# A fifth batch's keys and values computed early, at the border between two decoder layers

## The chip, the cores and the metric

The kernel runs on one core of one Trainium2 chip. A core has a matrix engine (TensorE, called PE in the profile; its weight loads are PEld), a vector engine (VectorE, DVE), an activation engine (ScalarE, ACT), a general engine (GpSimd, POOL) and a sync engine (SyncE, SP) that mostly issues transfers. Each engine works through its own queue in order, and semaphores tie the queues together. Sixteen DMA engines move data between the device memory (HBM) and the on-chip memories: SBUF with 128 partitions, and PSUM, in eight banks, into which PE writes. The metric is the device time of one execution, in microseconds; less is better.

## The reference

A decoder of two layers in single precision, on 16 batches of 112 tokens with 256 features; a context of 375 rows per batch feeds the cross-attentions. Cut to what matters here:

```python
x = x + attn0(ln(x))                      # layer 0: linear attention
x = x + xattn0(ln(x), ctx)                # layer 0: cross-attention
x = x + moe0(ln(x))                       # layer 0: top-2 of 16 experts, and a shared one
x = x + attn1(ln(x), W_qkv, W_out)        # layer 1: softmax self-attention, 16 heads of 64
x = x + xattn1(ln(x), ctx)                # layer 1: cross-attention, 8 heads of 64
x = x + moe1(ln(x))                       # layer 1: top-2 of 8 experts, with a capacity

def xattn1(x, context):
    xn = layer_norm(x, g1, b1); cn = layer_norm(context, g2, b2)
    q = xn @ Wq
    k, v = split(cn @ Wkv, 2)             # Wkv: 256 x 1024
    return softmax(q k^T / 8) v @ Wout + bout
```

The keys and values of xattn1 depend on the context and on weights alone, not on x. They can be computed at any time before the second cross-attention reads them.

## The kernel before

The whole decoder is one program in stages. Activations `x` stay in SBUF (112 tokens on the partitions, 16 batches); `xnT` holds the normalised, transposed input of the running stage, 128 x 2 x 1792. `w_all` is one large SBUF region, cut into weights by hand; its third part, from 2*WR, holds in turn the weights of layer 0's attentions, the key and value weights `Wkv` of xattn1, and the q, k and v weights of attn1.

**Batches computed ahead.** Four batches, `AHEAD` (line 359), have their keys and values for xattn1 computed during layer 0. The pieces are `c_ahead` (three PE transposes of the context for one half of its features, and an ACT evacuation with scale and bias), `k_ahead` (one of four key pieces: two matmuls of 375 columns, an ACT copy) and `v_ahead` (one of three value pieces: two matmuls of 512 columns, an ACT copy). After the last piece ACT's queue writes the result to device memory (`kd`, `vd`). `norm_ahead` normalises the context on DVE. A list `ahead` holds these pieces, and `take` puts some of them between the routing steps and the shared expert of layer 0, where PE would wait.

**The expert blocks.** Layer 0's expert rows are sorted into blocks of 128 rows. `blocks` (line 1143) runs 36 of them as a pipeline: `fetch` loads rows five blocks ahead, `turn` transposes, `up` multiplies, `turn_act` transposes the activation, `down` multiplies and scatters the rows back to device memory (`yo`) with an indirect transfer from POOL. `fetch` also starts the three weight loads of attn1, behind the rows of blocks 12, 17 and 22.

**The join.** Behind the 36 blocks every engine loads the number of blocks that the routing needs and branches (lines 1161 and 1162): only if there are more than 36, the conditional block runs the rest. Behind it, the first instructions of each engine wait for what went before, the scattered rows among it.

**Layer 1.** `combine` (line 1528) loads a batch's two expert rows per token, DVE adds them to `x`, `norm_one` normalises (DVE, POOL) and transposes (PE) them into `xnT`. After the first two batches come nine pieces of q, k and v projections, and then 32 units of self-attention. While they run, contexts and pieces for the first batch that is not in `AHEAD` are made ready.

**The second cross-attention.** `units` is a list of 32 half batches (four heads each). In each turn PE transposes the weights of the current half (`turned`), computes the scores of the next (`scores`: DVE takes the maxima, ACT the exponentials, DVE the reciprocals, POOL the division, line 1484), and multiplies by the values. Between these it makes what the next batch needs: if that is not in `AHEAD`, two `c_piece`, four `k_piece` and three `v_piece` (the same work as the pieces ahead, line 1421 on); if it is, two loads from `kd` and `vd` through SP (`k_load`, `v_load`).

**What sets the order.** Within a block `manual_schedule` the named engines run in the order of the code: PE and DVE in layer 0's routing and blocks, PE alone in layer 1. The other engines' queues, SP's transfers among them, are ordered by a planner at build time, from estimated durations and dependencies. `issue_after` keeps a transfer behind another one on the same queue.

## Time and profile before

| | us |
|---|---|
| median of 3 runs | 1604.29 |
| lowest and highest run | 1603.69, 1607.48 |
| the profiled execution's own time | 1611.35 |
| its span, first to last instruction | 1609.6 |

The mean granted clock of PE in the profiled execution is 0.973 of full speed. By the trace, the expert blocks run from 546.8 to 608.4 us, the self-attention from about 640 to 948, the second cross-attention from there to about 1314.

In the lines of the profile, PE's busy time comes with the number of its instructions; a single-precision matmul of the program shows as two. `L120` is the helper `mm_sum`, so matmuls are told apart by their tiles. A row of stretches gives for each stretch its length, the busy time of PE, PEld, DVE, ACT and POOL, the granted share of PE's clock, the mean busy share of the DMA engines, and GB/s. A row of the timeline gives start, duration, engine, line, operation, tiles, the number of instructions merged, and in brackets the idle time before and what ended it.

### The profile page before, as it was taken

The page shows a single profiled execution, that of the slowest core. Times are in us where ns is not written, and L with a number is a line of the kernel's source. Part 1 is how long each engine was busy: PE and PEld are TensorE (multiplying, and loading weights), DVE is VectorE, ACT ScalarE, POOL GpSimd, SP SyncE. Part 2 cuts the span into 40 slices and gives each one's busy share as a digit, 9 for nine tenths or more (in the row PEclk, how much of TensorE's full clock was granted, in tenths as well). Part 3 has the DMA queues.
Part 4 walks back from the last instruction along what each step waited for, and adds up shares of the span by engine and source line. Part 5 has one row for each costly group of instructions (what it writes and reads, how often), then busy time and mean ns, then how long its engine had stood idle before and what let it go on. Part 6 is the DMA issues. An engine that isn't in the chain of part 4 may idle for free.

```text
span 1609.6 us, 30346 instructions
## 1 busy us (share of the span) xinstructions
PE 1501.8 (93%) x11438; PEld 1127.5 (70%) x11438; DVE 964.1 (60%) x2649; ACT 577.9 (36%) x1437; POOL 483.1 (30%) x647
## 2 busy tenths in 40 slices
PE   7898999999988896899999989999999978999998
PEld 5776777777754585778888756666666657788786
DVE  6986777777762353976677655566575566342124
ACT  3441444444442252223333233343434323333332
POOL 5642122222115352323333344544445420000000
PEclk9999999999999897999999999999999988999999
DMA  6500322222224476200000010101010012344421
GB/s 170 143 10 21 94 67 65 67 65 65 64 76 158 130 231 214 54 24 1 1 1 2 20 56 10 49 20 48 19 30 30 1 53 79 137 178 157 147 89 48
DMA packets 84929, 116.52 MB, mean 72 GB/s; under 512 B 13433, under 2 KB 70946, under 8 KB 84778
## 3 DMA queue, kind: packets, MB, share of 16 engines
q1 hardware_dynamic: 78690, 98.25, 20.1%
q0 software_dynamic: 3312, 8.54, 1.6%
q10 hardware_dynamic: 2776, 7.72, 1.4%
q8 instruction: 95, 1.56, 0.4%
q14 instruction: 56, 0.46, 0.1%
HBM read 84.41 MB, written 22.08 MB: 66 GB/s over the span
## 4 chain that ended last, share of the span: by engine, by line
PE 76%; DVE 13%; POOL 4%; DMA 3%; issue 2%; another core or an unknown queue 1%; ACT 1%; SPq 0%; POOLq 0%; DVEq 0%; ACTq 0%
PE pT L120 49%; PE pT L785 3%; PE pT L1461 3%; PE pT L1493 2%; POOL pr L1484 2%; DVE mx L769 2%; PE pT L1509 2%; PE pT L803 2%; PE pT L767 2%; PE pT L1358 2%; PE pT L1393 2%; PE pT L1379 2%; PE pT L620 1%; DVE st L234 1%
## 5 line engine op out<-in xcount | busy, mean ns | idle before, releaser
L1484 POOL TENSOR_SCALAR pr<-pr,den 112x375 f32<-112x375 f32 x128 | 157.0, 1244 | 176.9 <-DVE den L1482 157.7
L120 PE MATMUL pT<-xnT,w_all 128*128 128x224 f32 (+2 forms) x800 | 165.3, 358 | 0.6 <-DVE xnT L269 0.5
L120 PEld LDWEIGHTS pT<-xnT,w_all 128*128 128x128 f32 x800 | 145.9, 197 | 10.2 <-issue 5.7
L794 ACT ACTIVATE pr<-pT 125x336 f32<-125x336 f32 x256 | 94.6, 456 | 126.3 <-PE pT L785 126.3
L769 DVE TENSOR_REDUCE mx<-pT 112x1 f32<-112x375 f32 x256 | 122.2, 539 | 11.3 <-PE pT L767 9.9
L1371 POOL TENSOR_TENSOR pr<-pr,den 112x448 f32<-112x448 f32 x64 | 59.9, 956 | 198.8 <-DVE den L1369 147.9
L120 PE MATMUL pT<-w_all 128*128 (+3 forms) x376 | 113.1, 453 | 1.7 <-ACT w_all L392 0.8
L120 PE MATMUL pT<-w_all,cT 128*125 128x256 f32 (+1 forms) x336 | 111.4, 475 | 0.0
L120 PE MATMUL pT<-cT,w_all 128*128 128x375 f32 x320 | 110.2, 486 | 0.0
L120 PE MATMUL pT<-w_all,xnT 128*112 128x256 f32 (+1 forms) x320 | 105.7, 477 | 1.9 <-ACT xnT L566 0.9
L120 PE MATMUL pT<-w_all,oT 128*112 128x256 f32 x448 | 106.4, 383 | 0.6 <-DVE oT L1400 0.6
L242 POOL TENSOR_SCALAR nr<-nmv 112x1 f32<-112x1 f32 x96 | 22.3, 232 | 273.7 <-DVE nmv L235 273.1
L1308 ACT COPY pT<-pT 112x448 f32<-112x448 f32 (+1 forms) x64 | 34.0, 532 | 170.9 <-PE pT L1493 88.3
L120 PEld LDWEIGHTS pT<-w_all 128*128 128x128 f32 (+2 forms) x376 | 70.2, 190 | 33.8 <-issue 4.6
L1473 ACT ACTIVATE pr<-pT,top 112x375 f32<-112x375 f32 x128 | 72.4, 572 | 56.8 <-DVE top L1472 54.4
L120 PEld LDWEIGHTS pT<-cT,w_all 128*128 128x128 f32 x320 | 59.3, 190 | 41.1 <-issue 5.8
L120 PEld LDWEIGHTS pT<-w_all,oT 128*112 128x112 f32 x448 | 75.7, 177 | 16.3 <-DVE oT L1400 1.0
L120 PE MATMUL pT<-first_in,w_all 128*128 128x192 f32 x512 | 86.6, 329 | 0.0
L120 PEld LDWEIGHTS pT<-first_in,w_all 128*128 128x128 f32 x512 | 84.4, 192 | 1.5 <-issue 0.3
L120 PEld LDWEIGHTS pT<-w_all,cT 128*125 128x125 f32 x336 | 61.1, 187 | 33.3 <-issue 22.7
L120 PEld LDWEIGHTS pT<-w_all,xnT 128*112 128x112 f32 x320 | 57.1, 183 | 35.8 <-issue 22.4
L1767 DVE SCALAR_TENSOR_TENSOR hT<-pT,vT,gt 128x192 f32<-128x192 f32 x64 | 26.7, 417 | 90.5 <-ACT gt L1766 90.4
(306 smaller groups left out, 3019.2 us busy)
## 6 DMA issues: line engine op xcount, KB each, us to landing
w_all<-in_L_ffn_w_c_fc_dram SPq DMA_DIRECT2D x12, 1024.0 KB
w_all<-in_L_ffn_w_gate_dram SPq DMA_DIRECT2D x12, 1024.0 KB
w_all<-in_L_ffn_w_c_proj_dram SPq DMA_DIRECT2D x12, 1024.0 KB
cx<-in_ctx_dram SPq DMA_DIRECT2D x32, 375.0 KB
kz<-kn SPq DMA_DIRECT2D x128, 46.9 KB
xg<-w_all SPq DMA_DIRECT2D x1, 5547.0 KB
xb<-xg SPq DMA_DIRECT2D x36, 129.0 KB
yb<-yo SPq DMA_DIRECT2D x16, 224.0 KB
```

Source lines behind the costliest of these rows:

```text
L120: mm(o, l, r, start=(i == 0), stop=(i == len(terms) - 1))
L767: mm(ps[i][:L, :S], qz[b % 2][r, g, :], kz[b % 2][r, g, :], start=True, stop=True)
L769: nc.vector.tensor_reduce(mx[b % 2][:, g, i, 16:17], ps[i][:L, :S], AX.X, ALU.max, negate=True)
L785: mm(pw[i][:KC, j * L : (j + 1) * L], kz[b % 2][r, g, j * KC : (j + 1) * KC], qm[r, :], start=True, stop=True,)
L794: nc.scalar.activation(pr[:, i, :], pw[i][:KC, : NKC * L], AF.Exp)
L803: mm(po[32 * i : 32 * i + 32, :L], va[b % 2][:, j, 4 * g + i, :], pr[:, i, j * L : (j + 1) * L], start=(j == 0), stop=(j == NKC - 1),)
L1308: nc.scalar.copy(dst, src)
L1358: mm(ps[k][:L, s * L : (s + 1) * L], q, kk, start=True, stop=True)
L1371: nc.gpsimd.tensor_tensor(pr[:, k], pr[:, k], bcast(den[:, k, :], L), ALU.mult)
L1461: mm(ps[2 * s + k][:L, :S], qTs[b // 2][rows(k), m, (b % 2) * L : (b % 2 + 1) * L], kTs[b][rows(k), m, :], start=True, stop=True,)
L1473: nc.scalar.activation(pr[:, i, :], ps[i][:L, :S], AF.Exp, bias=top[:, i : i + 1], scale=1.0, accum_out=den[:, i : i + 1],)
L1484: nc.gpsimd.tensor_scalar(pr[:, n, :], pr[:, n, :], den[:, n : n + 1], None, ALU.mult)
```

## The change

Batch 2 becomes the fifth batch computed ahead. It is not worked into the list `ahead`; its pieces are placed by hand.

- Its context is loaded by `ctx_ahead`, which already runs for the index 4 after the transposes of the third batch. It is normalised on DVE in turn 30 of the block pipeline, and transposed in turns 36 and 37, where no new block begins.
- The key and value weights are needed once more, and attn1's weights have replaced them in `w_all`. They are loaded a second time (1 MB), behind block 24's rows, into the last 1024 columns of each half of `xnT`, which nobody needs until layer 1 reaches those batches.
- Two key pieces stand behind the 36 blocks, ahead of the branch; two key pieces and the three value pieces stand behind the conditional block, in a region in which PE's order is the code's, ahead of layer 1. ACT's queue writes keys and values out, as for the other four.
- In the second cross-attention batch 2 is no longer projected but loaded, during batch 1, and the contexts that are fetched there are those of the other eleven batches.

```diff
-    AHEAD = (0, 4, 8, 12)
+    AHEAD = (0, 4, 8, 12, 2)
...
                 kap[0].tile([128, 2, S], F32, tag="acT", name="acT", bufs=1)
-                if i % 2
+                if i % 2 or i == 4
...
-        mm_sum(pk[:, :S], [(wkv_a[0][:, c, m * 128 : (m + 1) * 128], acTs[i][:, c, :]) for c in range(2)])
+        mm_sum(pk[:, :S], [(wkv_a[i // 4][:, c, m * 128 : (m + 1) * 128], acTs[i][:, c, :]) for c in range(2)])
...
-        mm_sum(pv[:KC, :], [(acTs[i][:, c, j * KC : (j + 1) * KC], wkv_a[0][:, c, 512:]) for c in range(2)])
+        mm_sum(pv[:KC, :], [(acTs[i][:, c, j * KC : (j + 1) * KC], wkv_a[i // 4][:, c, 512:]) for c in range(2)])
...
-        for i in range(len(AHEAD))
+        for i in range(4)
...
-            + [lambda i=i, c=c: c_ahead(i + 1, c) for c in range(2)] * (i + 1 < len(AHEAD))
+            + [lambda i=i, c=c: c_ahead(i + 1, c) for c in range(2)] * (i < 3)
...
+                    if j == 24:
+
+                        wkv_a.append(xnT[:, :, NT - 1024 :])
+                        with tc.issue_after(got.ins):
+                            nc.sync.dma_start(wkv_a[1], rows_of(t["L1_xattn_Wkv"]))
...
+                    if begin == 0 and n == stop - 6:
+                        norm_ahead(4)
+                    if begin == 0 and n in (stop, stop + 1):
+                        c_ahead(4, n - stop)
...
             blocks(0)
+            for m in range(2):
+                k_ahead(4, m)
         n_used = nc.values_load(used[0:1, 0:1], min_val=0, max_val=NB0)
         with tc.If(n_used > NB_MEAN):
...
+        with tc.manual_schedule(engines={mybir.EngineType.PE}):
+            for m in range(2, 4):
+                k_ahead(4, m)
+            for j in range(NKC):
+                v_ahead(4, j)
```

## The prediction

> **What bounds the kernel now.** I read the page first. TensorE (PE) is busy 93% of the span and carries 76% of the chain that ended last, so work taken off PE counts where PE sets the pace, and work put on it is free only where it stands idle.

> ```profile
> span 1609.6 us, 30346 instructions
> PE 1501.8 (93%) x11438; PEld 1127.5 (70%) x11438; DVE 964.1 (60%) x2649; ACT 577.9 (36%) x1437; POOL 483.1 (30%) x647
> ...
> PE 76%; DVE 13%; POOL 4%; DMA 3%; issue 2%; another core or an unknown queue 1%; ACT 1%; SPq 0%; POOLq 0%; DVEq 0%; ACTq 0%
> ```

> Then the stretches of the layers' border. PE works 1.24 us of the 14.9 us after the last expert block, and at half the clock for most of it; the next stretch starts at half clock too, with the DMA engines full.

> ```profile
> 608.40:623.30 14.90, 1.24 (x4) 0.58 (x4) 4.26 (x14) 0.47 (x1) 4.56 (x8) 0.59 0.43 135
> 623.30:640.00 16.70, 16.66 (x66) 14.16 (x67) 4.57 (x12) 2.80 (x5) 1.58 (x4) 0.85 1.03 369
> ```

> The timeline of PE and POOL says what the gap is, and the waits (us, times, longest) who holds it.

> ```profile
> 606.93 0.33 PE L1126 MATMUL pT<-call,sg 128*128 128x128 f32 x1
> 607.10 1.27 PE L1133 MATMUL pT<-w_all,aT 128*128 x4
> 620.98 0.61 PE L267 MATMUL pT<-call,xn 112*128 112x112 f32 x2 [12.61 <-DVE nmv L235]
> 622.22 0.63 PE L267 MATMUL pT<-call,xn 112*128 112x112 f32 x2 [0.64 <-DVE xn L238]
> 623.34 8.70 PE L120 MATMUL pT<-xnT,w_all 128*128 128x224 f32 x32 [0.48 <-DVE xnT L269]
> ```

> ```profile
> 610.40 0.96 POOL L1063 DMA_INDIRECT yo<-os,to  x1 [0.30 <-issue]
> ```

> ```profile
> SPq L1530 <- DMA yo<-os,to: 13.6, 1, 13.6
> ```

> The last scatter of expert rows lands at 613.16; every engine's first instruction behind the conditional block is released within 0.02 us of that. This is the join: nothing behind it starts earlier, whatever it depends on. Then come the gather (landed 616.66), adds, norm, and the first projections at 623.34.

> Last, the second cross-attention, cut from one batch's scores to those of two batches later. Odd lines end up with a batch whose successor is projected in place, even lines with one whose successor's keys and values are loaded (4, 8, 12).

> ```profile
> 980.20:1027.00 46.80, 46.80 (x285) 30.64 (x284) 24.62 (x59) 18.75 (x53) 21.03 (x20) 1.00 0.12 35
> 1027.00:1068.75 41.75, 38.77 (x256) 26.27 (x255) 21.51 (x54) 15.98 (x47) 21.00 (x20) 0.96 0.08 28
> 1068.75:1117.70 48.95, 48.95 (x299) 32.95 (x298) 34.69 (x115) 19.84 (x58) 21.54 (x20) 1.00 0.12 33
> 1117.70:1160.20 42.50, 40.62 (x263) 27.73 (x262) 23.05 (x59) 16.95 (x51) 21.00 (x20) 0.96 0.07 27
> 1160.20:1209.10 48.90, 48.90 (x299) 32.63 (x298) 33.75 (x112) 19.56 (x56) 21.48 (x20) 1.00 0.12 33
> 1209.10:1250.70 41.60, 39.65 (x266) 27.18 (x264) 23.46 (x62) 17.48 (x53) 21.22 (x20) 1.00 0.07 27
> ```

> PE is never idle where the successor is projected, and idle 2 to 3 us where it is loaded. The pieces that move are these (start, us):

> ```profile
> 981.65 0.86 PE L1430 MATMUL pT<-call,cx 125*128 125x125 f32 x6
> ...
> 985.59 2.69 PE L120 MATMUL pT<-cT,w_all 128*128 128x375 f32 x8
> 988.12 1.88 PE L120 MATMUL pT<-w_all,cT 128*125 128x512 f32 x4
> ...
> 1044.73 0.97 PE L1493 MATMUL pT<-call,pr 112*125 112x112 f32 x3 [0.63 <-POOL pr L1484]
> 1045.63 2.69 PE L1461 MATMUL pT<-kt,qt 64*112 64x375 f32 x8
> ```

> From start to start, six context transposes take 0.70 us, two key pieces 2.53, one value piece 1.75 (1.81 alone, 3.43 for two). One batch is 0.70 + 5.06 + 5.24 = 11.0 us of PE.

> **The change part by part.**

> 1. *Extra transfers among the expert blocks.* One more 1024 KB load of the key/value weights, issued by SP behind block 24's rows, and batch 2's context earlier. The three weight loads already there stand at 560.37, 568.51 and 576.64; around the last, two up-projections of a block take 1.11 and 0.96 us instead of 0.87, 0.33 together, and nothing else moves, since rows are fetched five blocks (8.1 us) ahead. I take 0.1; from 0 to 2.7 us (1 MB at the 380 GB/s of the border burst, were none of it covered).

> 2. *Normalising batch 2's context on DVE at block 30.* Three operations of 0.32 us. DVE idles 0.75 us in each 1.63 us block and each block's pieces are spread over four turns: 0, covered by that idle time; without it 0.96.

> 3. *Context transposes in the last two turns.* 0.70 us of PE and two ScalarE (ACT) evacuations of some 0.5 us (the neighbouring 128x375 copies take 0.47), between the last gated outputs. What they may delay is the last output on ACT (608.41 to 608.88), which POOL takes only at 610.40, as its scatters follow each other every 1.26 us. POOL is elsewhere 0.59 us behind ACT, so 0.93 us is cover. I take 0.1, up to 0.7.

> 4. *Two key pieces ahead of the join.* 2.53 us of PE from about 609.0 to 611.6, the copy by 612.1, then ACT's own load of the block count (0.47) and branch: about 1 us of cover before 613.16, since SP's first gather also waits for ACT to have passed. 0; if the order on ACT eats the cover, the join is up to 0.7 late.

> 5. *Two key and three value pieces behind the join.* PE passes a row of semaphore waits from 613.19 to about 614.3, then has 2.53 + 5.24 = 7.77 us of work ahead of the first transposes, which would be ready at 620.98 and 622.22. So this part is not fully hidden. PE's clock: after an idle stretch from 611.6 to 614.3 I count one granted-clock window at half, 3.41 us (the trace's half-clock stretches are multiples of it), that is 1.7 us lost. PE is through at 614.3 + 7.77 + 1.7 = 623.8, the four transposes and their copies take it to 624.8, 1.5 later than 623.34. But the projections now run at full clock: in the profile 623.34 to 628.19 was at half, 4.85 us, worth 2.4. Border: 1.5 - 2.4 = -0.9. Ends: clock never falls, -2.6; half clock through the whole stack (15.5 us instead of 9.5), +5.1.
> [...]

> 6. *Writing the keys and values out.* Two transfers of 750 KB from ACT's queue at about 619 and 624, into the burst (share 1.03) that loads the next weights. 1.5 MB at 380 GB/s ends it 3.9 us later, near 644; the first thing behind it on SP, batch 4's gathered rows, is used at 648.4. 0; from there on up to 3.9 if it isn't covered. ACT has nothing else between 609 and 626.8.

> 7. *Second cross-attention: batch 2 is loaded, not projected.* 11.0 us of PE go, but not as time. With little PE work a half batch waits for the scores' path: the last normalised weights came from POOL 8.1 and 9.2 us after their scores started (four times 1.24 us on POOL at its end). The pair at 3 has this shape already: 41.75 for 46.80, so -5.05. Ends: 42.50 for 46.80 gives -4.3; 41.60 for 48.90 gives -7.3, though that dense pair holds dispatch work that the first lacks. The half clock at 1045.63 is in 41.75. SP gets two more loads; the key buffer is free at 961.9, its scores come at about 989, the value buffer at 978.7 for about 1000; the next context fetch behind them has as long. Nobody waits.

> Sum: 0.1 + 0 + 0.1 + 0 - 0.9 + 0 - 5.05 = -5.75. The profiled execution took 1611.35 us (span 1609.6), 7 us over the median of the three runs, 1604.29. Profiled 1605.6; on the median's scale 1598.5.

> **Rivals.**

> A. *The border gives the gain back.* If the stack behind the join runs at half clock throughout, part 5 is +5.1 and the total 0.2 - 5.05 + 5.1: 1604.5. For it: in the profile half clock lasted 7.2 us past PE's return at 620.98. Against it: those first 2.3 us had two gaps, the stack has none. Between the ends lie times of 1601 to 1605.

> B. *The planner's queues cost more than is won, slower than before.* Behind the join only PE's order is written by hand; DVE, ACT, POOL and SP are ordered from estimated times, which the stack shifts. Its place is DVE's queue between 640 and 700, where PE already idles 7 us: four x_res adds of 3.51 us stand in front of a copy PE needs (648.50), and DVE waits 6.08 us for a context transfer at 683.01. One more stall of 6.08 makes 1604.6; it decides from 5.75 us of new PE idle time there, and two such stalls make 1610.7. Against it: that stage's own instructions do not change.

> C. *More than forecast.* No half-clock window behind the join (-1.7), and the light pair worth 1.7 us more, -6.75 where part 7's far end is -7.3: 1595.1. For it: the later pairs. Against it: their dense halves carry work that this one lacks, and the gap ahead of the stack is there.

> **How the numbers follow.** The forecast 0.46 (own range 1596 to 1601), A 0.24, B 0.16, C 0.14. What a measurement of this kernel can tell is 0.3%, 4.8 us: faster is below 1599.5, slower above 1609.1. Of the forecast's chance some 0.32 lies below 1599.5; with C 0.46. Slower is the half of B with more than one stall, 0.09. Within 0.3%: 0.45. The range 1594 to 1607 leaves out the end of C and the worse half of B.

> **What would show it.** Right: PE busy from about 609 to 611.6 and from 614.3 to near 624; first projections about 1.5 us later but done near 639; the pair of batches 1 and 2 about 41.8 us long with waits for POOL's pr; the gather still released by the scatter near 613. Wrong: a join past 614, PE's stack running past 627, PE idle between 640 and 700 above 9 us, block turns longer than 1.63 us after block 24.

## The result, and the profile after

The changed kernel takes 1625.07 us (median of 4 runs, 1623.25 to 1630.92) where the kernel before takes 1603.99 (median of 4, 1602.75 to 1607.48) on the same chip: a ratio of 1.0134, 95% interval 1.0103 to 1.0166. It is slower by 21 us; forecast was a gain of 5.75 and a range that ended at 1607.

Its profiled execution took 1623.59 us. That of before, at 1611.35, was 7 us over its own median, and the trace puts the difference ahead of the expert blocks, where the change adds no more than the load of batch 2's context: the first block's products begin at 548.2 before and at 538.9 after. So the two spans differ by 12.1 us only, and the comparison by stages has to leave that start out. Worked out from the starts and ends of the named instructions in both traces (us; the self-attention is counted to the start of the second half batch's scores):

| stage | before | after | difference |
|---|---|---|---|
| expert blocks, first product to last | 60.2 | 63.5 | +3.3 |
| border: end of the blocks to the first self-attention scores | 32.0 | 46.2 | +14.2 |
| self-attention | 318.8 | 320.4 | +1.6 |
| second cross-attention, first two halves | 21.1 | 22.1 | +1.0 |
| its pair of batches 1 and 2 | 46.8 | 45.1 | -1.7 |
| its pair of batches 3 and 4 | 41.8 | 44.7 | +2.9 |
| its other halves, and all behind | 540.8 | 540.9 | +0.1 |

The sum is +21.4; the medians differ by 21.1. Two thirds of it is the border; the light pair gained a third of its forecast, and its neighbour lost more than that.

From the page of the profile after. PE's share is the same 93% of a longer span, at 1513.3 us busy instead of 1501.8: the same 11438 matmuls took longer.

```profile
span 1621.7 us, 30350 instructions
PE 1513.3 (93%) x11438; PEld 1135.3 (70%) x11438; DVE 962.0 (59%) x2646; ACT 579.9 (36%) x1440; POOL 483.4 (30%) x647
```

The stretches of the profile after: the 14.9 us behind the last block, the next 14.7, the projections, and the two pairs. Columns as before: length, busy time of PE, PEld, DVE, ACT and POOL, granted share of PE's clock, DMA share, GB/s.

```profile
602.40:617.30 14.90, 10.52 (x29) 4.89 (x27) 0.00 (x0) 4.23 (x9) 2.05 (x3) 0.96 0.24 93
617.30:632.00 14.70, 1.75 (x5) 1.08 (x6) 4.81 (x15) 0.00 (x0) 2.21 (x5) 0.50 0.51 164
632.00:648.60 16.60, 16.60 (x68) 13.94 (x66) 4.09 (x12) 3.08 (x6) 1.58 (x4) 0.86 1.00 358
991.10:1036.16 45.06, 41.70 (x252) 28.27 (x251) 21.59 (x53) 16.06 (x47) 21.03 (x20) 0.89 0.14 43
1036.16:1080.84 44.68, 41.79 (x256) 28.45 (x255) 21.74 (x54) 16.05 (x47) 21.07 (x20) 0.89 0.07 26
```

In the first stretch PE works on batch 2, and DVE does nothing at all: layer 1 has not begun. In the second, layer 1 begins and PE stands idle, as it did in the first stretch of before. The gap was not filled, it was put off. In the pairs the granted clock is 0.89, where the light pair of before had 0.96.

The timeline of the profile after, of PE, SP, ACT and POOL, at the border:

```profile
602.28 2.69 PE L120 MATMUL pT<-acT,xnT 128*128 128x375 f32 x8
606.16 2.79 PE L120 MATMUL pT<-acT,xnT 128*128 128x375 f32 x8 [1.18 <-ACTq L1173]
608.79 5.31 PE L120 MATMUL pT<-xnT,acT 128*125 128x512 f32 x12
628.92 0.61 PE L267 MATMUL pT<-call,xn 112*128 112x112 f32 x2 [14.82 <-DVE nmv L235]
...
631.49 3.73 PE L120 MATMUL pT<-xnT,w_all 128*128 128x224 f32 x9 [0.48 <-DVE xnT L269]
...
622.45 5.16 SPq L1546 DMA_DIRECT2D yb<-yo  x4
...
609.49 0.35 ACTq L403 DMA_DIRECT2D kd<-ak  x1
...
614.75 0.50 ACTq L416 DMA_DIRECT2D vd<-av  x1
...
604.10 0.96 POOL L1063 DMA_INDIRECT yo<-os,to  x1 [0.30 <-issue]
623.09 0.61 POOL L1317 DMA_DIRECT2D bout<-in_L_xattn_bout_dram  x1 [18.03 <-DMA vd<-av]
```

Three things are to be seen. The key pieces behind the branch start at 606.16, 2.06 us after the last scatter was issued; by the trace it landed at 606.87. PE's stack is done at 614.1, at full clock (5.31 us for three value pieces, 1.77 each). And POOL is idle for 18.03 us ahead of its load of a bias vector (`bout`), which has nothing to do with batch 2, until the write of batch 2's values has landed. The gather of layer 1 goes out at 622.45, 18.3 us after the last scatter's issue; before it was 3.5. The waits of SP in that stretch say what holds the gather (us, times, longest), the longest first:

```profile
SPq L1546 <- DMA yo<-os,to: 14.1, 1, 14.1
SPq L1546 <- DMA vd<-av: 9.4, 1, 9.4
SPq L1546 <- DMA kd<-ak: 5.5, 1, 5.5
```

In order of time the scattered rows come first, as before, then 5.5 us more for the keys' write, then 9.4 more for the values' write. The last of these holds more than SP: by the trace the write of the values has landed at 622.25, and the queues of SP, ACT, POOL, PE and DVE all go on between 622.26 and 622.28. Why should a gather of expert rows wait for them? The tile `yb` lies in `a1`, the pool of tiles that is opened when layer 1 begins, over memory that the closed pools of layer 0 have used, `ahead` (batch 2's `ak` and `av`) among them. In this kernel a pool that says nothing else waits, at each engine's first use of it, for everything that touched the memory under it. The two writes read `ak` and `av`; so they were among it. That reading was tested on the chip.

### The profile page after: what moved, and what is told of

Same layout as the page of the kernel before. It is cut to its first block, busy times and chain, and to the rows that moved or that the text cites. A ratio compares the mean times of both kernels' runs of the same rounds, so it can differ in the third digit from the quotient of the medians.

```text
span 1621.7 us, 30350 instructions
## 1 busy us (share of the span) xinstructions
PE 1513.3 (93%) x11438; PEld 1135.3 (70%) x11438; DVE 962.0 (59%) x2646; ACT 579.9 (36%) x1440; POOL 483.4 (30%) x647
## 4 chain that ended last, share of the span: by engine, by line
PE 50%; DVE 5%; POOL 4%; DMA 1%; ACT 1%; issue 1%; SPq 0%; POOLq 0%; ACTq 0%; DVEq 0%
PE pT L120 35%; POOL pr L1500 3%; PE pT L1477 3%; PE pT L1509 2%; PE pT L1525 2%; PE pT L1374 2%; PE pT L1395 2%; PE pT L1409 2%; PE pT L1823 1%; DVE x_res L1549 1%; DMA cx<-in_ctx_dram 1%; ACT pr L1489 1%; PE pT L1446 1%; PE pT L1291 1%; PE pT L267 1%
## 5 line engine op out<-in xcount | busy, mean ns | idle before, releaser
L120 PE MATMUL pT<-xnT,w_all 128*128 128x224 f32 (+2 forms) x800 | 165.3, 358 | 0.6 <-DVE xnT L269 0.5
L120 PEld LDWEIGHTS pT<-xnT,w_all 128*128 128x128 f32 x800 | 145.9, 197 | 9.9 <-issue 5.4
L120 PE MATMUL pT<-w_all 128*128 (+3 forms) x376 | 113.1, 453 | 1.7 <-ACT w_all L392 0.8
L120 PE MATMUL pT<-w_all,oT 128*112 128x256 f32 x448 | 110.9, 394 | 0.6 <-DVE oT L1416 0.6
L120 PE MATMUL pT<-cT,w_all 128*128 128x375 f32 x304 | 106.0, 491 | 0.0
L120 PE MATMUL pT<-w_all,cT 128*125 128x256 f32 (+1 forms) x324 | 105.9, 471 | 0.0
L120 PE MATMUL pT<-w_all,xnT 128*112 128x256 f32 (+1 forms) x320 | 103.9, 472 | 1.7 <-ACT xnT L566 0.9
L120 PEld LDWEIGHTS pT<-w_all 128*128 128x128 f32 (+2 forms) x376 | 70.1, 190 | 33.7 <-issue 4.3
L120 PEld LDWEIGHTS pT<-w_all,oT 128*112 128x112 f32 x448 | 78.3, 183 | 18.1 <-DVE oT L1416 1.0
L120 PE MATMUL pT<-first_in,w_all 128*128 128x192 f32 x512 | 86.4, 329 | 0.0
L120 PEld LDWEIGHTS pT<-first_in,w_all 128*128 128x128 f32 x512 | 84.3, 192 | 1.5 <-issue 0.3
L120 PEld LDWEIGHTS pT<-cT,w_all 128*128 128x128 f32 x304 | 57.5, 194 | 39.7 <-issue 6.5
L120 PEld LDWEIGHTS pT<-w_all,xnT 128*112 128x112 f32 x320 | 56.5, 180 | 34.7 <-issue 22.4
L120 PEld LDWEIGHTS pT<-w_all,cT 128*125 128x125 f32 x324 | 58.7, 187 | 31.2 <-issue 20.7
```

Source lines behind the costliest of these rows:

```text
L120: mm(o, l, r, start=(i == 0), stop=(i == len(terms) - 1))
```

## The experiments

Chips differ (the kernel before has a median of 1604, 1615, 1606 and 1608 us on the four that were used), so each ratio is to runs of before on the same chip.

### 1. The pool waits tile by tile

```diff
-        lp = pool(ph, "a1", 2)
+        lp = pool(ph, "a1", 2, reuse_waits="tile")
```

The changed kernel with this one word: a tile of the new pool waits for those that used its own bytes.

> The changed kernel, but layer 1's pool of tiles is opened so that each tile waits for the earlier tiles that lay at its own place, instead of every engine's first use of the pool waiting for all that lay in the pools before. Theory 1 (the two writes of batch 2 hold back the pool that layer 1 opens, and with it the gather): the first gather is issued about 1 us after the last scatter has landed, instead of 15.6 us (622.45 against 606.87); the time falls by 13 to 16 us, to about 1610. Rival (the writes occupy the DMA engines or the queue, so the gather would be late in any case): the gather's rows still land after the value write, and the time stays within 4 us of 1625.

Measured: 1611.17 us (median of 10, 1607.87 to 1625.48), 0.9985 of before [0.9958, 1.0012]. The timeline at the border, of PE, SP and POOL:

```profile
621.12 5.31 PE L120 MATMUL pT<-xnT,acT 128*125 128x512 f32 x12
626.95 0.41 PE L267 MATMUL pT<-call,xn 112*128 112x112 f32 x2 [0.51 <-DVE xn L238]
...
629.38 5.82 PE L120 MATMUL pT<-xnT,w_all 128*128 128x224 f32 x21 [0.52 <-DVE xnT L269]
...
619.48 6.21 SPq L1546 DMA_DIRECT2D yb<-yo  x4
...
616.44 0.96 POOL L1063 DMA_INDIRECT yo<-os,to  x1 [0.30 <-issue]
```

The gather leaves 3.04 us after the last scatter's issue, while PE is still ahead of the value pieces; PE's idle time behind them is 0.51 us, not 14.82. The border is 30.8 us long, 46.2 in the profile after. The value write, issued at 627.1, is still there and holds nobody. So some 15 us of the border were the pool's waits.

### 2. The same word in the kernel before

> The kernel before with the same one word at layer 1's pool, as the control for the run above. There the last thing that the pool waits for is the scatter that the gather needs anyway: 1604, within 3 us. If this alone made the kernel faster by 10 us, the run above would say nothing of the writes.

Measured: 1615.55 us, 0.9997 [0.9983, 1.001]; border 30.5 us (32.0 in the profile of before). In time the word is worth nothing there, because nothing under the pool was later than the rows that the gather needs anyway. But it changes who is released when. In the kernel before, ACT's queue stands until the scatter has landed (613.16); with the word it has gone on to layer 1's first copy at 613.13 and waits there for PE, 3.4 us before the scatter lands (616.55). So in the profile of before the pool released the engines together when the scatter landed, and that looked like the branch. The trace of before could have told them apart: the branch itself (L1162) is over at 608.7 us or earlier on PE and DVE and at 609.5 on ACT, and the instructions that are released at 613.16 carry lines of layer 1 (L267, L1533, L1338).

### 3. The value write in two

```diff
-            nc.scalar.dma_start(vd[AHEAD[i]], akv[i])
+            for r in (slice(0, 112), slice(112, KC)) if i == 4 else (slice(0, KC),):
+                nc.scalar.dma_start(vd[AHEAD[i]][r], akv[i][r])
```

> The changed kernel, with batch 2's value write of 125 rows split into one of 112 rows and one of 13. In the profile the key write (128 rows) took 2.06 us from first to last packet with 30.5 us of packet time, the value write (125 rows) 6.39 us with 31.7: some 15 and some 5 packets in flight. Theory 2 (a transfer of 125 rows is spread over few DMA engines): the 112 rows take about 2 us, the value write lands some 4 us earlier, and since the gather waits for it the time falls by 3.5 to 5 us, to about 1620.5. Rival (device memory takes the value write slowly, or other traffic is in its way): the same 6 to 7 us and 1625.

Measured: 1626.37 us, 1.0066 [1.0049, 1.0083]. The gather follows the value write's issue by 4.3 us instead of 7.7, and the border is 41.7 us long, 4.5 less than after. The changed kernel was not run on this chip, so the border alone tells what the division is worth. In the trace of the changed kernel the key write (128 rows) is through in 2.06 us and the value write (125 rows, about as many bytes) in 6.39, though their packets took 30.5 and 31.7 us in all: on average 15 packets are under way at a time in the first and 5 in the second. With the value write in two, both parts are through in 3.00 us. How a row count comes to its number of packets under way was not shown: 128 rows and 125 are the two that were counted.

### 4. The gain alone: load batch 2, leave out its own keys and values

```diff
-        own = [b for b in range(B) if b not in AHEAD]
+        LOADED = AHEAD + (2,)
+        own = [b for b in range(B) if b not in LOADED]
...
-            nc.sync.dma_start(kTs[b], kd[b])
+            nc.sync.dma_start(kTs[b], kd[b if b in AHEAD else 0])
```

> The kernel before, with nothing added at the border: in the second cross-attention batch 2 loads batch 0's keys and values instead of projecting its own, so batch 2's keys and values are left out. It shows what that half of the change is worth alone. The prediction's part 7: 5.05 us less, 1599. Theory 3 (half-clock windows after the starved half eat part of it, as in the changed kernel's profile, where the pair of batches 1 and 2 took 45.06 us instead of 41.75): 1.7 to 5 us less, 1599 to 1602.5, and the pairs of stretches differ from run to run by whole windows.

Measured: 1611.0 us, 0.9968 [0.995, 0.9986], or 4.2 us less than 1615.22 by the medians; the pair of batches 1 and 2 takes 42.9 us for 46.8.

### 5. The changed kernel again

> The changed kernel once more, beside the runs it is compared with on this chip. If the loss is the kernel's own, it is again 1.3% (21 us) over the kernel before, with the gather of layer 1 issued about 18 us after the last scatter, and one to three half-clock windows among the light halves of the second cross-attention. If the 21 us belonged to the chip of the first comparison, it is nearer to the 0.7% (11 us) that the kernel with the divided value write showed.

Measured: 1617.52 us (median of 10, 1614.74 to 1632.59), 1.0084 [1.006, 1.0107]: slower again, by 11 us, not 21, so nearer to the second of the two expectations. Its profile has the same border (46.7 us) and the same wait, but the pairs take other times:

```profile
987.58:1030.42 42.84, 39.87 (x251) 27.12 (x250) 21.31 (x53) 16.06 (x47) 21.04 (x20) 0.92 0.15 46
1030.42:1072.22 41.80, 38.80 (x255) 26.14 (x254) 21.59 (x54) 16.07 (x47) 21.04 (x20) 0.96 0.07 28
```

The same instructions in the same order: 42.84 and 41.80 us at clock 0.92 and 0.96, against 45.06 and 44.68 at 0.89. From the first self-attention scores to the start of the last feed-forward stage this run takes 695.6 us, with 48.5 us of them at half clock by the trace's record of the clock; the profile after takes 706.2 with 73.1; before took 702.4 with 48.9. So at nearly equal half-clock time the change wins 6.8 us there, and the profile after, with 24 us more at half clock, is 10.6 us longer than this run. Both the border and the clock speak in the 21 us.

### 6. No writes

```diff
-        if m == 3:
+        if m == 3 and i < 4:
             nc.scalar.dma_start(kd[AHEAD[i]], akv[i])
...
-        if j == NKC - 1:
+        if j == NKC - 1 and i < 4:
             nc.scalar.dma_start(vd[AHEAD[i]], akv[i])
```

> The changed kernel without batch 2's two writes to device memory; batch 2 then loads batch 0's keys and values, so its own result leaves out its own keys and values. The pool of layer 1 keeps its default waits. Theory 1 (the new pool waits for all that touched the memory under it, the writes last): the gather is issued right after the last value copy on ACT, 1 us behind the value stack's end and not 7.7 us behind the value write's issue; the run is 7 to 8 us shorter than the changed kernel, and still 6 to 8 us longer than the one with waits by tile, which doesn't wait for the stack at all. Rival 2 (the stack and ACT's copies alone hold the border, the writes are hidden): no gain, 1.2 to 1.3% over before.

Measured: 1611.23 us (median of 8), 1.003 [1.0013, 1.0048], 6.3 less than the changed kernel on the same chip; the border is 38.5 us, 8.2 shorter than there. The waits of SP and of POOL around the border:

```profile
SPq L1546 <- DMA yo<-os,to: 14.1, 1, 14.1
SPq L1546 <- ACT av L414: 7.2, 1, 7.2
```

```profile
POOL bout L1317 <- ACT av L414: 10.0, 1, 10.0
```

With no write to wait for, the gather and the bias vector wait for the last copy into `av` (which ends at 615.67; the gather leaves at 615.69). The rest of the border's loss has the same cause one step earlier: 8.2 us came from the writes and 7.7 (38.5 against 30.8 in experiment 1) from the stack with its copies.

### 7. Waits by tile, and the second weight load in four

Experiment 1 also had one long turn among the blocks. Its timeline and the waits of PE there:

```profile
590.05 0.27 PE L1131 MATMUL pT<-call,sg 128*128 128x128 f32 x1
590.16 0.60 PE L1138 MATMUL pT<-w_all,aT 128*128 x2
592.52 0.41 PE L1115 MATMUL pT<-call,xb 128*128 128x128 f32 x2 [1.76 <-DMA xb<-xg]
```

```profile
PE pT L1115 <- DMA xb<-xg: 1.8, 1, 1.8
```

```diff
-                    if j == 24:
-
-                        wkv_a.append(xnT[:, :, NT - 1024 :])
+                    if j in (24, 25, 26, 27):
+                        if j == 24:
+                            wkv_a.append(xnT[:, :, NT - 1024 :])
+                        cols_of = slice((j - 24) * 256, (j - 23) * 256)
                         with tc.issue_after(got.ins):
-                            nc.sync.dma_start(wkv_a[1], rows_of(t["L1_xattn_Wkv"]))
+                            nc.sync.dma_start(wkv_a[1][:, :, cols_of], rows_of(t["L1_xattn_Wkv"])[:, :, cols_of])
```

> Waits by tile, and the second load of the key and value weights (1 MB behind block 24's rows) divided into four loads of 256 KB behind the rows of blocks 24 to 27. If the one long turn among the blocks (4.24 us instead of 1.63 with waits by tile) comes from the 1 MB that stands ahead of a block's rows on the queue, no turn is over 2.3 us and the run is about 2.5 us shorter than with waits by tile: 0.9965 of before. If rows come late for another reason, the long turn stays.

Measured: 1608.03 us (median of 7, 1596.14 to 1614.4), 0.9995 [0.996, 1.0029]. The turn in question is 1.63 us long again, so the megabyte ahead of a block's rows was its cause; in the kernels with the undivided load it took 1.98 to 4.29. The border is 28.9 us. The time, though, was not the expected 0.9965: the profiled run's two pairs take 45.1 and 44.7 us at clock 0.89. The granted clock of its seven runs goes from 0.968 to 0.979, and their time against it, from 1614.4 down to 1596.1.

### 8. All three

The same as 7, with every value write of the five batches (the expectation names batch 2's alone) and every load of a context in rows 0 to 111 and 112 to 124.

```diff
-        nc.sync.dma_start(cx, t["ctx_1024"][b].rearrange("(c p) d -> p c d", p=KC))
+        for r in (slice(0, 112), slice(112, KC)):
+            nc.sync.dma_start(cx[r], t["ctx_1024"][b].rearrange("(c p) d -> p c d", p=KC)[r])
...
-            nc.scalar.dma_start(vd[AHEAD[i]], akv[i])
+            for r in (slice(0, 112), slice(112, KC)):
+                nc.scalar.dma_start(vd[AHEAD[i]][r], akv[i][r])
```

> The same, with batch 2's value write and every load of a context divided into rows 0 to 111 and 112 to 124, since 125 rows as one transfer took 6.39 us where 128 rows of the same bytes took 2.06. If these transfers still cost time at the border and in the self-attention (DVE waits 0.8 to 4.2 us for a context, 16 to 22 us in all), 1 to 6 us shorter than without the division: 0.993 to 0.996 of before. If they are hidden from PE, the same as without it.

Measured: 1595.04 us (1593.47 to 1596.25), 0.9927 [0.9907, 0.9947]. This beats both kernels.

### 9. The border alone

The changed kernel, where the lists of the second cross-attention use `AHEAD[:4]`, so that batch 2 is projected there as before.

> The changed kernel up to the border, its two writes included, but batch 2's keys and values are projected in the second cross-attention all the same, as before. It prices the border alone. Theory 1: the border is 14 to 15 us longer than before, the pair of batches 1 and 2 takes 46.8 us, and the run is 15 us over before, 1.009 to 1.010. The rival, that part of the changed kernel's loss sits in the second cross-attention itself (its light pair longer than the dense one), would leave this kernel under 10 us over before.

Measured: 1624.06 us, 1.0105 [1.0079, 1.013]: 16.6 us over before, border 46.6 us. The stretches of its two pairs:

```profile
987.29:1034.09 46.80, 46.80 (x285) 30.64 (x284) 24.59 (x59) 18.74 (x53) 21.03 (x20) 1.00 0.12 34
1034.09:1079.07 44.98, 42.00 (x255) 28.59 (x255) 21.75 (x54) 16.05 (x47) 21.03 (x20) 0.89 0.08 26
```

The border carries the loss by itself. And the second row is a light pair that the change does not touch, at 44.98 us: a light pair took about 45 us in either place (45.06 for batches 1 and 2 in the profile after), while the dense pair, with PE never idle, took 46.80 here and in the profile of before.

### 10. The context loads in two, in the kernel before

> A control for the divided loads: the kernel before with every load of a context divided into rows 0 to 111 and 112 to 124. If the divided loads alone made the kernel with all three edits fast, this one gains as much, 0.996 or less. If what it won is the change itself with its border mended, this one stays within 0.3% of before.

Measured: 1602.51 us (median of 10) against 1607.51, 0.9974 [0.9958, 0.999]. Among the waits of the kernel before stands this row of DVE; here it is gone altogether.

```profile
DVE cx L238 <- DMA cx<-in_ctx_dram: 22.1, 11, 3.5
```

So by the medians the divided loads give 5 of the 13 us that all three edits win on this chip. How they come to PE is not shown. The self-attention takes 313.5 us here and 318.8 in the profile of before, but it is 315.9 to 320.6 in the traces with undivided loads and 315.7 in that of experiment 11, and it holds 4.4 us at half clock here, 13.7 in before: an estimate from these two is that 4.6 of the 5.3 us are the clock's. Of DVE's 22.1 us PE's own waits between 640 and 960 us show 1.1: its one wait of that stretch for a normalised batch (L267, for `xn`) is 1.4 us long instead of 2.5.

### 11. All three again, on another chip

> The kernel with all three edits on another chip: 0.991 to 0.995 of before again if its gain is its own; up to 0.999 if it met a good position of the half-clock windows in four runs.

Measured: 1594.54 us (1592.31 to 1599.47), 0.9928 [0.9904, 0.9952]; 8.0 us less than experiment 10 on the same chip. That is what the change wins with its border mended, the divided value writes of the other four batches included, which experiment 10 lacks. The pairs of the profiled run:

```profile
966.92:1009.64 42.72, 39.75 (x251) 27.01 (x250) 21.50 (x53) 16.05 (x47) 21.00 (x20) 0.92 0.13 46
1009.64:1051.45 41.81, 38.83 (x256) 26.18 (x255) 21.38 (x54) 16.06 (x47) 21.00 (x20) 0.96 0.08 28
```

### 12. All but the context loads

Experiment 11 without the divided loads of contexts; the value writes of all five batches stay divided.

> The same without the divided loads of contexts: waits by tile, the weight load in four, the value write in two. If the context loads are hidden from PE, it equals the kernel with all three edits; if they cost PE's time in the self-attention, it is 2 to 6 us slower than that.

Measured: 1603.83 us (median of 6, 1596.74 to 1611.07), 0.997 [0.9938, 1.0001], 9.3 over experiment 11. Experiment 10 accounts for about 5 of it. The rest goes with the clock, 0.968 to 0.976 in these runs and 0.975 to 0.980 in those of experiment 11. Whether the divided loads keep the light halves clear of long half-clock stretches, or nine runs of the kernel with all three edits were lucky, stays open.

## Why the prediction was wrong, point by point

**The join, and part 6 (writing the keys and values out): the step that failed.** I read "every engine's first instruction behind the conditional block is released within 0.02us" as a property of the branch, and so looked for what the change does to the time at which the scatter lands. The release came from the pool that opens behind it. The pieces behind the branch started at 606.16, 0.7 us before the scatter had landed; what waited was every first use of layer 1's tiles, for whatever lay under them. Part 6 priced the writes at "0; from there on up to 3.9", with "the first thing behind it on SP, batch 4's gathered rows". The first thing behind them was all of layer 1: 8.2 us by the writes, 7.7 by the stack and its copies (from the borders of experiments 5, 6 and 1). The question I did not ask of the row of waits was which resource each engine's first instruction takes, and who used it last.

**Part 5 (the stack).** Predicted: border -0.9, with ends -2.6 and +5.1. Measured: +14.2. With the pool's wait gone the border is 30.8 us (experiment 1), and with the weight load divided as well 28.9, 27.9, 28.2 and 28.2 (experiments 7, 8, 11, 12). Against 30.5 in experiment 2, the kernel before with the same word, that is +0.3 and -1.6 to -2.6, within the ends; against 31.9 in experiment 10 the four are -3.0 to -4.0, but that may take in what the word shortens by itself. The -2.4 for projections at full clock came true in those four (from the first projection to the first scores 14.6 us, 17.0 before), not in experiment 1 (16.2), where one half-clock window of 3.4 us begins with the projections. The +1.5 for a late stack did not, since the stack starts 2 us after the last scatter's issue and not when it has landed. The half-clock window that I put into the stack was an estimate, and it did not come: the pieces ran at full clock, with 1.18 us of idle time ahead of them where I had counted 2.7. Whether idle time of PE brings such a window, and how much of it, no run shows; the gaps ahead of the one in experiment 1 are 0.51, 1.09 and 0.52 us.

**Part 7 (the light pair).** The mechanism was right, the size too sure: -5.05, ends -4.3 and -7.3. Measured: -1.7 (first chip), -4.0 (the next), and -4.9 in experiment 1. 41.75 was the figure of one trace. The same pair has one, two or three half-clock windows of 3.4 us by the trace's record of the clock, and takes 41.9, 42.7 to 42.9 or 45.0 to 45.1 us accordingly. The unchanged pair of batches 3 and 4 goes the same way, from 41.8 to 44.7 (45.0 in experiment 9), and that I had not counted as a term at all.

**Part 1 (the extra load).** Predicted 0.1, from 0 to 2.7. The turn behind it was 0.8 us long in excess in the profile after, 0.35 in experiment 5 and 2.6 in experiment 1. The far end had been worked out right; the small value came from neighbouring loads that happened to be covered. Of the +3.3 us of the blocks in the table, 1.8 lie in the first block, whose products run at half clock in the profile after; they do so in experiment 10 too, the kernel before with its context loads divided, and do not in experiments 1 and 3, which have the change, so that is no part of it. 1.1 lie in the later turns, 0.4 behind the last of them.

**Parts 2 to 4.** The turn with the normalisation took 1.76 us instead of 1.63 (forecast 0); from the last block's first products to the end of its last ones 2.52 us pass instead of 2.13, with the transposes between (forecast 0.1, up to 0.7); the two key pieces ahead of the branch delayed nothing that showed. All three lie within 0.3 us of the forecast.

**The rivals.** A came nearest in kind, a border that gives the gain back, but by another mechanism and at three times its price. B named a wait in a planner's queue as the way to a slower kernel, 6 us each between 640 and 700; the self-attention grew by 1.6 only. Neither had a wait of layer 1 on the work that was being put under it. With that mended (experiment 11), the gain of 8.0 us over experiment 10 is nearer to that of rival C, 9.2, than to the forecast's 5.75; it comes with the divided value writes of four more batches, which neither counted.

## What to carry to other kernels

Before work is moved into a gap at a change of stage, ask what releases the first instruction of the next stage on each engine, and whether it is data or memory: an opening pool that waits for all that lay under it makes every late reader of that memory, an outgoing transfer included, a barrier for everything behind (here 8.2 us by the transfers and 7.7 by the stack with its copies). If the release times of all engines agree to 0.02 us, look for such a resource, and see whose lines the released instructions carry. And a saving in a stretch where PE is paced by another engine has a spread: take its time from several traces, since the clock may hold a few windows more or less (here one pair took 41.9 to 45.1 us).

## What the runs showed of the hardware

```profile
1009.80 2.85 PE L1477 MATMUL pT<-kt,qt 64*112 64x375 f32 x8
```

```profile
1003.97 2.20 PE L1477 MATMUL pT<-kt,qt 64*112 64x375 f32 x8
```

At full clock they take 1.52 us. In both the clock falls with no gap of PE over 0.84 us ahead of it in the pair. For one kernel on one chip the granted clock of ten runs lay between 0.961 and 0.973 and the time between 1614.74 and 1632.59 us (experiment 5), so, by an estimate from these runs, up to 18 us of such a kernel's time may go with its half-clock windows; that the clock is the whole of that spread was not tried.
